# Gated scan and a sparse mixture of experts on one core: one chunk's statistics ahead of the others, two roots on GpSimd, and another weighting of the planned order

## The chip, the cores and the metric

The kernel runs on one core of a Trainium2 chip. The metric is the device time of one execution in microseconds (us). Before the change it is 376.28, the median of three runs that lie between 375.01 and 378.33. Besides these there is one execution under the hardware profiler; it took 377.76, and every duration of a single instruction below comes from it.

Engines go by these names: PE is TensorE's matmul pipeline and PEld its weight loads, DVE is VectorE, ACT is ScalarE, POOL is GpSimd, SP is SyncE, which here only issues transfers.

## The reference

The input `x` is 16 sequences of 256 tokens with 128 channels, 4096 rows of float32. Two sub-layers follow each other, both with a normalisation in front and one behind:

```
x = x + layernorm(scan(layernorm(x)))
x = x + layernorm(moe(layernorm(x)))

scan:  i = sigmoid(x Wi' + bi);  r = sigmoid(x Wr' + br)
       a = exp(-8 softplus(lambda) r);  g = sqrt(1 - a^2) (i x)
       h[t] = a[t] h[t-1] + g[t]          # along the 256 tokens

moe:   scores = sigmoid(x gate_w')         # 32 experts
       ids = top 4 of scores + e_bias;  w = scores[ids] / sum
       out = sum over e of combine[e] (silu(x w1[e]) * (x w3[e])) w2[e]   # 128 -> 96 -> 128
```

The four normalisations have no scale or offset. The reference computes all 32 experts for all tokens; only four of them have a weight that isn't zero.

## The kernel before

**Chunks.** The 4096 rows are eight chunks of 512, each four tiles of 128 rows. Every chunk goes through `mix` (from L578), which does the first sub-layer and the router: normalise (L589, on ScalarE or VectorE), transpose with TensorE (`swap`, L442), two gate matmuls (L600), tanh, exp, square, relu and square root on ScalarE (L607 to L625), products on VectorE (L621, L627), the scan along the tokens (L633, `hs`), transposes back (L641), the inner normalisation and the residual (L647), a second normalisation (`hn`), transposes again (`sw_c`), the router's logits (L675) and the top four.

**Statistics.** `norm` computes mean and variance for the first normalisation and is used twice: for chunk 0 alone, and for chunks 1 to 7 together. `rsqrt` (L385) computes 1/sqrt(var + eps) from them by nine small VectorE operations (L394 to L410), a shift of the bits and two Newton steps. A name in the list `POWS` would take another branch, which does it with an addition and a power on GpSimd (L391, L392); the list is empty. The roots are named by the normalisation and its chunk: `a0` and `a1` for the two of `norm`, `b` and a chunk for the one behind the scan, `c` and a chunk for the one ahead of the router, `d` for the last.

**Two ways through the experts.** Chunks 0, 2, 3 form group 0, chunks 4, 5, 6 group 1. Their rows are sorted by expert through DRAM: `send` (L499) has GpSimd scatter each tile of 128 rows four times by row numbers (L507, 16 indirect DMAs a chunk), SP loads the sorted blocks back (`loads`, L908), and `experts` (L912) works through 68 blocks per group in pieces of four: transposes (xT, L924), gate and up matmuls (gu, L938), silu on ScalarE (L944), product on VectorE (L946), transposes (aT, L954), down matmuls (y_ps, L964), a copy (yb, L973) and a store of 256 KB. Then `fetch` has GpSimd gather what belongs to each token (yk, L1044, 48 indirect DMAs a group) and `combine` adds it, normalises and stores (ff, L1080, L1082).

Chunks 1 and 7 aren't sorted. `dense` (L1089) computes all experts for them, in 24 tiles of 128 intermediate columns each: dg and du (gate and up) and dw (the combine weights spread over the columns) at L1111, silu on ScalarE (L1120), two products on VectorE (L1123, L1131), and the sum acc (L1135), whose matmuls all go into one bank. `finish` (L1142) transposes the sum back, normalises it, adds the residual (res) and stores it.

**The order of the work.** Each of these functions is a generator, and each `yield` announces one step: an engine, a planned duration in us, for ScalarE also the set of its function tables. `Order.run` (from L37) steps through all of them with a model of the engines' free times and writes the program's order from it: of the steps that can begin first (within `SOON` of each other on an engine) it takes the one with the smallest due time, where a ScalarE step that needs another table set counts `STAY` later. A step marked `EITHER` goes to ScalarE or VectorE, whichever the plan has finish it first; its two durations are given with it, and for the normalisations and the copies VectorE's are the constants `LND` and `CPD`. Due times come from the list `pieces` (L1180 on): `LEAD + STEP * c` for `mix` of chunk c, and from it those of `send`, `experts`, `find` and `fetch`; for the dense tiles `DUE`, `DDUE` and `DUE2`, and `KEEP` is how many dense tiles of the last chunk may be planned before the last expert piece of group 1 has begun (L1094). A step `UNTIL` waits in the plan for a time set by another step. What the generators call is issued in this order on PE, DVE, ACT and SP; each engine then runs its own list in order and waits for others by semaphores.

GpSimd's indirect DMAs have a pacing beside the data they need: `in_pace` (L489) makes each wait for the last matmul that the plan has `AHEAD` us or more earlier.

At the end, all engines load the flag `more` (L1233 on), which tells whether an expert has more rows than the planned blocks; a branch around the extra blocks follows.

Of the kernel before, what the change touches and what calls it, by code (L numbers as in the profile page):

```python
# [11 lines left out]
I32 = mybir.dt.int32  # L12
U32 = mybir.dt.uint32
AF = mybir.ActivationFunctionType
ALU = mybir.AluOpType
# [4 lines left out]
EPS = 1e-5  # L20
K = 4
GROUPS = ((0, 2, 3), (4, 5, 6))
DENSE = (1, 7)
# [5 lines left out]
PE, DVE, ACT, POOL, SP, TIME = "pe", "dve", "act", "pool", "sp", "time"  # L29
# [7 lines left out]
class Order:  # L37
# [37 lines left out]
    def due(self, rank, step):  # L75
        due, n = rank
        if isinstance(due, dict):
            due = due.get(step[0], due[None])
        return due + STAY * self.switches(step), n

    def run(self, pieces):
# [8 lines left out]
        while live:  # L90
# [14 lines left out]
            if kind in (PE, DVE, ACT, POOL, SP):  # L105
                soon = [r for r in ready if r[3][0] == kind and r[0] <= begin + SOON]
                begin, _, p, step = min(soon, key=lambda r: self.due(r[1], r[3]))
# [19 lines left out]
                live.remove(p)  # L127


POWS = ()  # L130
POOLW = 0.9
RATE = 1.29
AHEAD = 3.0
READ = 0.0
LAST = 2
TINY = 0.07
SOON = 0.1
STAY = 6.0
LEAD, STEP, PACE = 38.0, 13.0, 0.6
DUE = 70.0  # L140
DDUE = 1.0
DUE2 = 200.0
LND, CPD = 1.7, 0.9
FLY2 = 3
KEEP = 6
MORE = 20
REGS = 3
SBANKS = 6
# [2 lines left out]
SLOT, UNTIL = "slot", "until"  # L151
# [3 lines left out]
def tile_gated_scan_then_moe(  # L155
# [30 lines left out]
    nc = tc.nc  # L186
# [3 lines left out]
    N = B * T  # L190
    TPC = 4
    CH = TPC * P
# [6 lines left out]
    NW = [min(n, t * K // P + MORE) for n, t in zip(NB, TG)]  # L199
    QB = 4  # L200
# [178 lines left out]
    def rsqrt(rstd, var, pool, name):  # L379

        shape = [P, rstd.shape[1]]
        if name in POWS:  # L385
            v = pool.tile(shape, F32, tag="newt_v", name=f"nv_{name}")
            yield POOL, POOLW
            nc.gpsimd.tensor_scalar(v, var, EPS, None, ALU.add)
            nc.gpsimd.tensor_tensor(rstd, v, mhalf.to_broadcast(shape), ALU.pow)
            return  # L390
        v = pool.tile(shape, F32, tag="newt_v", name=f"nv_{name}")  # L391
        t = pool.tile(shape, F32, tag="newt_t", name=f"nt_{name}")  # L392
        yield DVE, TINY
        nc.vector.tensor_scalar(v, var, EPS, None, ALU.add)  # L394
        yield DVE, TINY
        nc.vector.tensor_scalar(
            t.bitcast(I32), v.bitcast(I32), 1, None, ALU.arith_shift_right
        )
        yield DVE, TINY
        nc.vector.tensor_scalar(  # L400
            rstd.bitcast(I32), t.bitcast(I32), -1.0, float(0x5F1FFFF9), ALU.mult, ALU.add
        )
        k = 0.703952253
        for square, plus in ((-1.0, 2.38924456), (-0.5 * k**3, 1.5 * k)):
            yield DVE, TINY
            nc.vector.scalar_tensor_tensor(t, rstd, square, rstd, ALU.mult, ALU.mult)
            yield DVE, TINY
            nc.vector.tensor_tensor(t, t, v, ALU.mult)
            yield DVE, TINY
            nc.vector.scalar_tensor_tensor(rstd, t, plus, rstd, ALU.add, ALU.mult)  # L410

    def moments(src, name, pool):

# [26 lines left out]
    times = {}  # L440
# [48 lines left out]
    def in_pace(ins):  # L489

        old = [b for at, b in beats if at <= order.now - AHEAD]
        if old:
# [6 lines left out]
    def send(g, cg):  # L499

        c = GROUPS[g][cg]
        yield UNTIL, lambda: times["rows", c][0] if ("rows", c) in times else None
        _, rows, hn = times["rows", c]
        for j in range(TPC):
            for k in range(K):
                yield POOL, RATE
                ins = nc.gpsimd.indirect_dma_start(  # L507
                    out=rows_in[g],
                    out_offset=bass.IndirectOffsetOnAxis(ap=rows[:, j, k : k + 1], axis=0),
                    in_=hn[:, j, :], in_offset=None,  # L510
                )
                apart(ins, f"in_{g}")
                in_pace(ins)
                sent[g].append(ins)
        times["sent", g] = order.now
        yield TIME, 2.5
        give("hn")
# [5 lines left out]

    def norm(chunks):

        for c in chunks:
            yield DVE, 1.1
            stats = small.tile([P, TPC, 6], F32, tag="stats_a", name=f"st_a{c}")
            for j in range(TPC):
                nc.vector.bn_stats(stats[:, j, :], x_all[:, c * TPC + j, :])  # L530
            for j in range(TPC):
                nc.vector.bn_aggr(mv_a[:, c * TPC + j, :], stats[:, j, :])
        span = slice(chunks[0] * TPC, (chunks[-1] + 1) * TPC)
        yield from rsqrt(rstd_a[:, span], mv_a[:, span, 1], const, f"a{chunks[0]}")
        yield DVE, TINY
        nc.vector.scalar_tensor_tensor(
            shift_a[:, span], mv_a[:, span, 0], -1.0, rstd_a[:, span], ALU.mult, ALU.mult
        )
        for c in chunks:
            times["normed", c] = order.now  # L540
# [337 lines left out]
    def loads(g, begin, end):  # L878

        yield UNTIL, lambda: (  # L880
            times["sent", g] if len(sent[g]) == len(GROUPS[g]) * TPC * K and g in tables else None
        )
        yield TIME, 2.5
        lists, _ = tables[g]
        for q in range(begin, end, QB):
            nb = min(QB, end - q)
            if (q - begin) % (QB * RB) == 0:
                n = min(QB * RB, end - q)
                yield SLOT, "regs"
                yield SP, 1.0  # L890
                _, rows = nc.values_load_multi_w_load_instructions(
                    lists[0:1, 0, q : q + n], engines={ET.SP}, min_val=0,
                    max_val=E * TG[g] - P,
                    skip_runtime_bounds_check_because="a block lies within its expert's rows",
                )
                yield PE, 0.6
                _, es = nc.values_load_multi_w_load_instructions(
                    lists[0:1, 1, q : q + n], engines={ET.PE}, min_val=0, max_val=E - 1,
                    skip_runtime_bounds_check_because="an expert's number",
                )  # L900
                for i in range(n):
# [187 lines left out]
    def dense(d, k):  # L1089
# [3 lines left out]
        _, hT = times["hT", c]  # L1093
        if d == len(DENSE) - 1 and k >= KEEP:  # L1094
            yield UNTIL, lambda: 0.0 if began[-1] * QB >= NW[-1] else None
# [75 lines left out]
    def spans(g, cg):  # L1171

        n = LAST if (g, cg) == (NG - 1, len(GROUPS[g]) - 1) else TPC
        return [(j, n) for j in range(0, TPC, n)]
# [2 lines left out]
    w1_f, w3_f = (w13[:, i].rearrange("h e i -> h (e i)") for i in range(2))  # L1177


    pieces = [(LEAD + STEP * c, mix(c)) for c in range(N // CH)]  # L1180
    pieces.append((0, norm(range(1))))
    pieces.append((-1, decays()))
    pieces.append((LEAD + STEP, norm(range(1, N // CH))))
    for g, chunks in enumerate(GROUPS):
        pieces += [(LEAD + STEP * c, send(g, cg)) for cg, c in enumerate(chunks)]
        full = LEAD + STEP * (chunks[-1] + 1)
        read = full + PACE * NW[g] + READ
        pieces.append((0, table(g)))
        pieces.append((0, loads(g, 0, NW[g])))
        pieces += [  # L1190
            (full + PACE * q, experts(g, q, NW[g])) for q in range(0, NW[g], QB)
        ]
        pieces += [
            (read + STEP * (cg + (j + n) / TPC), combine(g, cg, j, n))
            for cg in range(len(chunks)) for j, n in spans(g, cg)
        ]
        pieces += [(full + STEP * (cg + 1), find(g, cg)) for cg in range(len(chunks))]
        pieces += [
            (read + STEP * (cg + j / TPC), fetch(g, cg, j))
            for cg in range(len(chunks)) for j in range(TPC)  # L1200
        ]
    for d, c in enumerate(DENSE):
        pieces += [
            ({PE: 400 + d * UB + k, None: (DUE2 if d == len(DENSE) - 1 else DUE + DDUE * d * UB) + DDUE * k}, dense(d, k)) for k in range(UB)
        ]
# [13 lines left out]
    def step(piece, steps=None):  # L1219
# [60 lines left out]
```

## Time and profile before

| what | us |
|---|---|
| median of three runs | 376.28 |
| the profiled execution | 377.76 |
| its span, from the first to the last instruction | 376.1 |
| PE busy (1423 instructions) | 305.8, 81% |
| DVE busy (1252) | 290.7, 77% |
| ACT busy (376) | 201.6, 54% |
| POOL busy (220) | 195.4, 52% |
| mean granted clock of TensorE | 0.927 |

| where | us from the start |
|---|---|
| chunk 0's statistics end, its shift begins | 6.75, 17.31 |
| second chunk's first tanh | 32.72 |
| first dense tile (dg) | 56.34 |
| first send of rows | 66.30 |
| first expert transposes of group 0, its last down matmuls | 143.99, 223.92 |
| first gather of group 0, last | 229.82, 300.15 |
| last down matmuls of group 1 | 298.15 |
| first gather of group 1, last | 303.16, 363.09 |
| last matmul ends | 357.1 |
| last store issued, end of the span | 371.48, 376.1 |

The first table says that TensorE and VectorE are both busy for about four fifths of the span and that no engine is full all the time. The second table gives the stages, and a stage is what has to be read: which engine is full in it, and which wait ends last. Matmul records are pipelined, so that PE's busy time is not that of a TensorE at its peak. The granted clock is the share of full speed that the throttle allows TensorE; by slices it falls to 0.5 between 36 and 60 us.

In a line of the timeline the columns are the start, the duration, the engine, the source line, the operation, the tile written and those read, the number of instructions, and in square brackets the idle time of the engine before it with what ended that. In a table by stretches each engine has its busy us, with the number of instructions in brackets, in the order PE, PEld, DVE, ACT, POOL, and behind them the granted clock, the DMA share and GB/s.

### The profile page before, as it was taken

Reading aid. Unit: us, or ns where it says so; the run is one execution under the profiler, and the core shown is the slowest. Engines: PE = TensorE matmul, PEld = TensorE weight load, DVE = VectorE, ACT = ScalarE, POOL = GpSimd, SP = SyncE. Lnnn points to the kernel's source line nnn. Section 1 sums busy time; section 2 is a strip of 40 time slices with the busy share of each in tenths; the row PEclk is TensorE's granted clock in tenths of the full one; section 3 lists DMA queues with packets and bytes.
Section 4 is the critical chain, followed back from the end, with each engine's and each line's share of the span. In section 5 each row is a group of like instructions: output and inputs, shape, how many; then the busy total and the mean of one; then the engine's idle time right before and its main releaser. Section 6 shows DMA issues by size and latency. Waiting matters only on the chain.

```text
span 376.1 us, 6098 instructions
## 1 busy us (share of the span) xinstructions
PE 305.8 (81%) x1423; PEld 199.2 (53%) x1423; DVE 290.7 (77%) x1252; ACT 201.6 (54%) x376; POOL 195.4 (52%) x220
## 2 busy tenths in 40 slices
PE   1095479799999998888889989877999999999900
PEld 0051254354543446777889956766999644444300
DVE  6955996989899998877874799637367488796993
ACT  2289897688677415457565546545466523141210
POOL 5000000772777727656737504776377767777750
PEclk9998657699999999899999999999699999999975
DMA  6906678362111124455545255667374522122231
GB/s 150 315 0 183 195 207 200 99 195 84 45 56 49 56 72 141 140 161 173 160 133 155 75 166 158 181 182 196 89 200 121 161 69 78 52 56 77 56 101 31
DMA packets 78856, 47.16 MB, mean 125 GB/s; under 512 B 15296, under 2 KB 75744, under 8 KB 78816
## 3 DMA queue, kind: packets, MB, share of 16 engines
q1 hardware_dynamic: 53808, 25.05, 24.3%
q0 software_dynamic: 6144, 12.60, 11.8%
q10 hardware_dynamic: 18864, 9.08, 8.2%
q8 instruction: 13, 0.21, 0.2%
q14 instruction: 27, 0.22, 0.2%
HBM read 23.76 MB, written 22.94 MB: 124 GB/s over the span
## 4 chain that ended last, share of the span: by engine, by line
PE 62%; DVE 12%; issue 5%; ACT 3%; POOL 2%; DMA 1%; DVEq 0%; POOLq 0%
PE gu L938 12%; PE acc L1135 10%; PE dg L1111 8%; PE y_ps L964 8%; PE du L1111 8%; PE aT_ps L954 4%; PE xT_ps L924 4%; PE dw L1111 2%; PE pl L675 2%; POOL yk L1044 2%; DMA yk<-rows_out,slots 1%; DVE a L1131 1%; DVE a L1123 1%; PE pr L600 1%; PE sw_c L448 1%
## 5 line engine op out<-in xcount | busy, mean ns | idle before, releaser
L507 POOL DMA_INDIRECT rows_in<-hn,rows x96 | 94.9, 988 | 113.2 <-DVE tot L481 60.8
L1044 POOL DMA_INDIRECT yk<-rows_out,slots x96 | 95.7, 996 | 54.8 <-issue 17.4
L938 PE MATMUL gu<-w,xT 128*128 x272 | 53.8, 336 | 7.9 <-issue 6.4
L1120 ACT ACTIVATE a<-dg 128x512 f32<-128x512 f32 x48 | 28.4, 596 | 49.7 <-PE dg L1111 49.2
L1135 PE MATMUL acc<-a,w_all 128*128 128x512 f32 x96 | 50.5, 617 | 3.3 <-DVE a L1131 1.4
L938 PEld LDWEIGHTS gu<-w,xT 128*128 128x128 f32 x272 | 44.6, 194 | 12.4 <-issue 7.7
L1111 PE MATMUL dg<-hT,w 128*128 128x512 f32 x96 | 50.7, 614 | 0.0
L1111 PE MATMUL du<-hT,w 128*128 128x512 f32 x96 | 50.0, 606 | 0.0
L946 DVE TENSOR_TENSOR act<-act,gu 128x192 f32<-128x192 f32 x68 | 23.0, 349 | 23.0 <-ACT act L944 22.5
L964 PE MATMUL y_ps<-w_sb,aT 96*128 x272 | 36.2, 280 | 5.3 <-issue 3.2
L1131 DVE TENSOR_TENSOR a<-a,dw 128x512 f32<-128x512 f32 x48 | 32.5, 681 | 9.1 <-PE dw L1111 8.6
L964 PEld LDWEIGHTS y_ps<-w_sb,aT 96*128 96x128 f32 x272 | 34.5, 196 | 8.5 <-issue 7.5
L1123 DVE TENSOR_TENSOR a<-a,du 128x512 f32<-128x512 f32 x48 | 32.4, 678 | 4.9 <-ACT a L1120 3.3
L944 ACT ACTIVATE act<-gu 128x192 f32<-128x192 f32 x68 | 22.0, 330 | 25.8 <-PE gu L938 21.6
L973 ACT COPY yb<-y_ps 128x512 f32<-128x512 f32 x34 | 19.9, 586 | 23.3 <-PE y_ps L964 22.3
L1135 PEld LDWEIGHTS acc<-a,w_all 128*128 128x128 f32 x96 | 17.1, 195 | 23.9 <-DVE a L1131 9.2
L1111 PEld LDWEIGHTS dg<-hT,w 128*128 128x128 f32 x96 | 18.3, 196 | 19.0 <-issue 17.3
L1111 PEld LDWEIGHTS du<-hT,w 128*128 128x128 f32 x96 | 17.7, 195 | 15.5 <-issue 14.0
L954 PE MATMUL aT_ps<-ident,act 128*96 128x128 f32 x136 | 20.4, 279 | 2.3 <-issue 1.6
L370 ACT COPY aT<-aT_ps 96x512 f32<-96x512 f32 x29 | 16.6, 583 | 9.4 <-PE aT_ps L954 8.1
L1054 DVE TENSOR_TENSOR yk<-yk,wk 128x512 f32<-128x512 f32 x24 | 16.5, 688 | 6.2 <-DMA yk<-rows_out,slots 6.0
L370 ACT COPY xT<-xT_ps 128x512 f32<-128x512 f32 x29 | 16.7, 588 | 7.0 <-PE xT_ps L924 6.1
(215 smaller groups left out, 520.9 us busy)
## 6 DMA issues: line engine op xcount, KB each, us to landing
xb<-rows_in SPq DMA_DIRECT2D x136, 64.0 KB
rows_out<-yb ACTq DMA_DIRECT2D x34, 256.0 KB
rows_in<-zeros SPq DMA_DIRECT2D x8, 512.0 KB
w<-in_L_ffn_w_dram SPq DMA_DIRECT2D x8, 384.0 KB
x_all<-in_L_attn_x_dram SPq DMA_DIRECT2D x8, 256.0 KB
w_all<-in_L_ffn_w_dram SPq DMA_DIRECT2D x4, 384.0 KB
w_sb<-in_L_ffn_w_dram SPq DMA_DIRECT2D x4, 384.0 KB
rows_in<-hn,rows POOLq DMA_INDIRECT x96
```

The lines of the kernel that those rows point to most:

```text
L370: (nc.vector.tensor_copy if kind == DVE else nc.scalar.copy)(dst, src)
L507: ins = nc.gpsimd.indirect_dma_start(out=rows_in[g], out_offset=bass.IndirectOffsetOnAxis(ap=rows[:, j, k : k + 1], axis=0), in_=hn[:, j, ...
L938: nc.tensor.matmul(pg[:, b, :], lhsT=xT[:, (h + b) * P : (h + b + 1) * P], rhs=w13[:, :, bass.ds(e, 1), :].rearrange("h s o i -> h s (o i) ...
L946: nc.vector.tensor_tensor(act[:, h : h + m, :], act[:, h : h + m, :], pg[:, :m, I : 2 * I], ALU.mult)
L954: nc.tensor.transpose(pa[:I, b * P : (b + 1) * P], act[:, b, :], ident)
L964: ins = nc.tensor.matmul(py[:, b, :], lhsT=aT[:, b * P : (b + 1) * P], rhs=w2_sb[:, bass.ds(e, 1), :].rearrange("i o h -> i (o h)"), start ...
L1044: ins = nc.gpsimd.indirect_dma_start(out=yk[:, k, :], out_offset=None, in_=rows_out[g], in_offset=bass.IndirectOffsetOnAxis(ap=rows[:, j, ...
L1111: ins = nc.tensor.matmul(ps, lhsT=lhsT, rhs=rhs, start=True, stop=True)
L1120: nc.scalar.activation(a, pg, AF.Silu)
L1123: nc.vector.tensor_tensor(a, a, pu, ALU.mult)
L1131: nc.vector.tensor_tensor(a, a, pw, ALU.mult)
L1135: nc.tensor.matmul(accs[d], lhsT=w2_all[:, k, :], rhs=a, start=(k == 0), stop=(k == UB - 1))
```

## The change

Eleven constants of the plan and three pieces of code differ.

- `rsqrt`: the roots of `b1` and `c1`, chunk 1's two inner normalisations, go to GpSimd (`POWS`), with a planned 1.4 instead of 0.9. A name in the new list `ATONCE` (`a0`, chunk 0's root) has its nine operations issued in one step of 1.7, where each was a step before, between which the plan could put others.
- `norm` of chunks 1 to 7 waits in the plan until chunk 0's shift is written.
- Chunk 7's `mix` is due at 200 (`MIXD`) instead of 38 + 13 x 7 = 129.
- `AHEAD` is 5 instead of 3.
- `STEP` 11 instead of 13, `DUE` 62 instead of 70, `DDUE` 2 instead of 1, `SOON` .12 instead of .1, `STAY` 8 instead of 6.
- `LND` 1.1 instead of 1.7, `CPD` .7 instead of .9: VectorE is planned to be quicker at normalisations and copies.
- `KEEP` 0 instead of 6.
- `LATER` is 0 and adds nothing.

```diff
-POWS = ()
-POOLW = 0.9
+POWS = ("b1","c1")
+ATONCE = ("a0",)
+POOLW = 1.4
 RATE = 1.29
-AHEAD = 3.0
+AHEAD = 5.0
+MIXD = 200.0
+LATER = 0.0
...
-SOON = 0.1
-STAY = 6.0
-LEAD, STEP, PACE = 38.0, 13.0, 0.6
-DUE = 70.0
-DDUE = 1.0
+SOON = 0.12
+STAY = 8.0
+LEAD, STEP, PACE = 38.0, 11.0, 0.6
+DUE = 62.0
+DDUE = 2.0
...
-LND, CPD = 1.7, 0.9
+LND, CPD = 1.1, 0.7
...
-KEEP = 6
+KEEP = 0
...
     def rsqrt(rstd, var, pool, name):
...
-        yield DVE, TINY
-        nc.vector.tensor_scalar(v, var, EPS, None, ALU.add)
-        yield DVE, TINY
...
+        def steps():
+            nc.vector.tensor_scalar(v, var, EPS, None, ALU.add)
+            yield
...
+        if name in ATONCE:
+            yield DVE, 1.7
+            for _ in steps():
+                pass
+            return
         yield DVE, TINY
+        for _ in steps():
             yield DVE, TINY
...
     def norm(chunks):
 
+        if chunks[0]:
+            yield UNTIL, lambda: times.get(("normed", 0))
...
-    pieces = [(LEAD + STEP * c, mix(c)) for c in range(N // CH)]
+    pieces = [
+        (MIXD if c == DENSE[-1] else LEAD + STEP * c, mix(c)) for c in range(N // CH)
+    ]
```

In the program that the planner writes with these, 30 normalisations of 128x128 and 14 copies of 128x512 have moved from ScalarE to VectorE, ScalarE has 24 loads of function tables instead of 27, and all 24 dense tiles of chunk 7 stand behind the experts of group 1 on TensorE, where before the sums of three stood ahead of the last of them. Of chunk 7's `mix`, the transposes and the logits stand later among the experts. Chunk 7's last addition (res) and its store stand behind the load of `more` and a branch; before, they stood ahead of it.

More of the change, by code (lines that the diff above doesn't have):

```diff
@@ L392, in rsqrt @@
         t = pool.tile(shape, F32, tag="newt_t", name=f"nt_{name}")
-        yield DVE, TINY
-        nc.vector.tensor_scalar(v, var, EPS, None, ALU.add)
-        yield DVE, TINY
-        nc.vector.tensor_scalar(
-            t.bitcast(I32), v.bitcast(I32), 1, None, ALU.arith_shift_right
-        )
-        yield DVE, TINY
[L400 to L404, printed above, removed]
-            yield DVE, TINY
[L406 to L410, printed above, removed]
+        def steps():
+            nc.vector.tensor_scalar(v, var, EPS, None, ALU.add)
+            yield
+            nc.vector.tensor_scalar(
+                t.bitcast(I32), v.bitcast(I32), 1, None, ALU.arith_shift_right
+            )
+            yield
+            nc.vector.tensor_scalar(
+                rstd.bitcast(I32), t.bitcast(I32), -1.0, float(0x5F1FFFF9), ALU.mult, ALU.add
+            )
+            k = 0.703952253
+            for square, plus in ((-1.0, 2.38924456), (-0.5 * k**3, 1.5 * k)):
+                yield
+                nc.vector.scalar_tensor_tensor(t, rstd, square, rstd, ALU.mult, ALU.mult)
+                yield
+                nc.vector.tensor_tensor(t, t, v, ALU.mult)
+                yield
+                nc.vector.scalar_tensor_tensor(rstd, t, plus, rstd, ALU.add, ALU.mult)
+        if name in ATONCE:
[3 more added lines that the diff above has]
+            return
+        yield DVE, TINY
+        for _ in steps():
+            yield DVE, TINY
     def moments(src, name, pool):
@@ L1190, in tile_gated_scan_then_moe @@
         pieces += [
-            (full + PACE * q, experts(g, q, NW[g])) for q in range(0, NW[g], QB)
+            (full + PACE * q + LATER * g, experts(g, q, NW[g])) for q in range(0, NW[g], QB)
         ]
```

## The prediction

> **What bounds the kernel now.** First the end, in the chain of waits followed back and the timeline, since a time is decided there; then the busy time by stretches, to see which engine carries each stage.
>
> ```profile
> 229.82 0.98 POOL L1044 DMA_INDIRECT yk<-rows_out,slots  x1 [16.29 <-DMA xb<-rows_in]
> ...
> 266.82 0.95 POOL L1044 DMA_INDIRECT yk<-rows_out,slots  x1 [3.21 <-PE y_ps L964]
> ...
> 303.16 0.94 POOL L1044 DMA_INDIRECT yk<-rows_out,slots  x1 [2.06 <-PE dw L1111]
> ...
> 363.09 0.95 POOL L1044 DMA_INDIRECT yk<-rows_out,slots  x1 [0.30 <-issue]
> ...
> 371.03 0.42 DVE L1080 TENSOR_TENSOR ff<-ff,x_all 128x256 f32<-128x256 f32 x1 [0.94 <-ACT ff L377]
> 371.48 0.37 SPq L1082 DMA_DIRECT2D out_dram<-ff  x1
> ```
>
> These are the first gather of group 0, one that was held, the first and the last of group 1, and the end. The last expert block's y_ps of group 1 begins at 298.15; its result has to be copied, stored and landed, and 5.0 us later the first of 48 gathers goes. The 48 take 59.9 (1.25 each), the last sums and norm 8.4, and the span ends 4.6 after the last store, when it has landed. TensorE runs beside this: from 298.15 it has 56.25 us of dense tiles of chunk 7 at full clock and ends them at 357.1, 58.95 for 56.25. It is the second, nearly as late, way to the end: chunk 7's normalisation ends at 364.3, 7.2 after its last matmul.
>
> ```profile
> 20.00:40.00 20.00, 12.78 (x36) 5.81 (x36) 11.25 (x41) 19.33 (x31) 0.00 (x0) 0.86 0.37 99
> 60.00:80.00 20.00, 17.25 (x55) 7.92 (x54) 16.47 (x91) 12.57 (x25) 10.65 (x11) 0.79 0.46 134
> 100.00:120.00 20.00, 19.62 (x61) 8.33 (x60) 19.18 (x91) 16.51 (x21) 15.12 (x17) 1.00 0.16 52
> 300.00:320.00 20.00, 20.00 (x52) 8.88 (x51) 16.68 (x46) 6.31 (x12) 13.89 (x14) 1.00 0.28 73
> 360.00:376.00 16.00, 0.00 (x0) 0.00 (x0) 9.82 (x49) 1.75 (x4) 3.12 (x4) 0.56 0.21 58
> ```
>
> Columns: busy PE, PEld, DVE, ACT, POOL, then granted clock. ScalarE is full at 20 to 40, TensorE from 80 to 140 and again from 300, with VectorE 0.8 us from full at 100 to 120; after 360 TensorE is idle. So the end is y_64 of group 1 (298.15) plus the longer of two tails.
>
> **The change, part by part.** *Start of chunk 0.*
>
> ```profile
> 17.31 0.16 DVE L536 SCALAR_TENSOR_TENSOR shift_a<-mv_a,rstd_a 128x4 f32<-128x4 f32 x1
> 17.51 1.65 ACT L377 ACTIVATE xn<-x_all,shift_a,rstd_a 128x128 f32<-128x128 f32 x4 [6.77 <-DVE shift_a L536]
> 20.76 3.19 ACT L377 ACTIVATE xn<-x_all,shift_a,rstd_a 128x128 f32<-128x128 f32 x8 [0.45 <-DVE shift_a L536]
> ```
>
> Chunk 0's statistics are ready at 6.75, yet its shift comes at 17.31, since its root's nine small operations are mixed among the other chunks' statistics. In one piece, behind the decay operations: shift near 9.8, 7.5 earlier. The others' statistics wait for it and their shift moves from 20.54 to about 24.2. ScalarE fills its 6.8 idle with chunk 0's gates, but the second chunk needs the others' shift: its first tanh, at 32.72, I place at 30.8, a gain of **2**. Bounds: 3.7 lost (all later chunks follow the late shift) to 7.5 gained (all follow chunk 0). The mixing steps also release 22 weight loads and zero fills on SP, five per chunk (L621 to L650), so these come as much earlier; chunk 7 has none left to move.
>
> *Roots of chunk 1 on GpSimd.* Two pairs of operations replace 18 on VectorE, 1.76 per root at the 0.2 us steps in which such chains run. No row shows a power; GpSimd's nearest are a memset at .10, a 128x32 copy at .92, and an indirect DMA at 1.71. A pair costs .2 to 3.4: 1.6 gained to 1.7 lost per root, on the latency of a dense chunk whose tiles are not due yet. I take 0, the copy's row (2 x .92) being equal to what goes. GpSimd is idle for 60.8 before its first send (66.30), so that hides them; behind them stand the sends, late if a root waits beyond that point.
>
> [...]
>
> *ScalarE to VectorE.* The planned prices move 30 normalisations (128x128: .48 each on ScalarE; on VectorE 16 of hn are busy 4.4, .27 each) and 14 copies (.59 against .69): VectorE gets 30 x .27 + 14 x .69 - 18 x .2 = +14, of which 5.6 stand ahead of the first gated product L946 of group 0 and about 7 ahead of group 1's end. ScalarE loses three table loads of 1.283 (27 to 24), but between the second chunk's first tanh and the first dense silu it has seven in both. The cover is VectorE's idle time: it is busy 75.66 of the 84 us from 60 to 144, so 8.3 are free for 5.6. At nothing then; without the cover, 5.6.
>
> *TensorE's order.* This is the main term. Nothing is removed; pieces move behind the experts. At full clock (dense gate, up and down tiles .86 each, the small dw .22, transposes .435 per four, logits .83) the work ahead of group 0's first expert transposes falls by 2.15, ahead of group 0's last y_ps by 6.4, and ahead of group 1's last y_ps by **8.4** (215.7 to 207.3): chunk 7's transposes and logits go later, all its 24 dense tiles too, where now three have their sums in before group 1 ends. TensorE is the busy engine there, so y_64 goes from 298.15 - 8.4 - 2 = 287.75. What left comes behind it: 56.25 + 8.4 = 64.65.
>
> *More slack for indirect DMAs.* Group 0's 48 gathers take 73.3 against 59.9 for group 1's, and 9.6 of that are waits for a PE instruction planned too close, the held row above among them. With 5 instead of 3 us between, they shrink; but group 0's gathers gain slack here, not the end: the first of group 1 is already bound by 298.15 + 5.0. At nothing; if the last gather of group 0 stays where it is (300.15), the first of group 1 goes at 294.8 at the earliest instead of 292.75, 2.0 lost. Of group 1's own gathers all but 1.8 and .9 of the waits are the .3 of an issue.
>
> *Program end.* In the changed order chunk 7's last addition and store stand behind the load of the flag `more` and a branch; now ff's last store is the last before it. No row has a branch. The store costs from .37 (one issue) to 4.62 (SP first waits until ff's store has landed, as the end of the span does). I take **2.5**, midway, since nothing nearer shows.
>
> *Sum.* GpSimd's way: first gather 287.75 + 5.0 = 292.75, last 352.7, last store 361.1, with two additions of chunk 7 mixed in (.35 each) 361.8. TensorE's way: 64.65 x 58.95/56.25 = 67.75, ending at 355.5; normalised 7.2 later, 362.7, added (.7) 363.4. The later one, plus 2.5, plus 4.62: a span of 370.5. The profiled execution took 377.76 for a span of 376.1, 1.66 around it: 372.2. It lies .4% above the median of the runs (376.28), so **370.7** for a median.
>
> **The rivals.** (a) *Chunk 0's lead carries through*: the tiles follow chunk 0 by 7.5 instead of 2. For it: ScalarE's 6.77 idle. Against: the others' shift later, and the granted clock near .5 at 36 to 60. Both ways to the end move 5.5: 365.2.
>
> (b) *Holes instead of a shorter stage*: the dense tiles that leave the expert stage filled gaps in it (TensorE is 17.4 to 17.8 of 20 at 160 to 200), and half of the 8.4 is not got. y_64 at 291.95; TensorE's way then decides: 291.95 + 67.75 + 7.2 + .7 + 2.5 + 4.62 = 374.7, a median of 374.9. What left must still be done later, which takes the gain back.
>
> (c) *VectorE becomes the bound, slower than before*: at 100 to 140 it has .8 to 1.0 idle in 20, and the 5.6 that are put ahead of the first gated product delay every expert block; the tiles that left then make holes only. It decides as soon as more than 5.6 of the 8.3 idle cannot be used, that is when fewer than 5.6 fall between the added operations. y_64 at 298.15 - 2 + 5.6 = 301.75; 67.75 + 7.2 + .7 + 2.5 + 4.62 behind it: 384.5, a median of 384.7.
>
> (d) *The slack does not do what it says*: 119 gathers and sends wait for TensorE now, 117 in the changed order, so they can be held as before. It costs the 2.0 above on GpSimd's way, .4 on the sum, and lies within the forecast.
>
> **How the numbers follow.** Forecast .47 (367 to 373.5 by the ends of the program-end term, 2.1 either side, and rival d), (a) .12, (b) .22, (c) .19. The range takes in (a) and (b) and reaches to (c): 361 to 384; outside remain some .12 above and .04 below. A measurement of this kernel tells about 1% from no change, 372.5 to 380.0: faster .42 + .12 + .03 = .57, same .05 + .17 = .22, slower .02 + .19 = .21.
>
> **What would show it.** Right: chunk 0's shift near 9.8 and the second chunk's first tanh near 31; y_64 of group 1 near 288; the last gather near 353; last matmul near 355; a store behind the branch 2 to 3 us after ff's. The groups must show waits of a gather for y_ps or dw below the 9.6 of group 0. Wrong: idle TensorE between pieces at 140 to 280 with y_64 above 292 is (b); VectorE at 20 of 20 from 60 to 140 with the first expert transposes later than 143.99 is (c); a GpSimd power of over 3 us, or sends later than 66.30, overturns the second part; a TensorE clock below 1.00 at 300 to 355 stretches the longer tail.

## The result and the profile after

The changed kernel takes 378.24 us, the median of 14 runs (376.83 to 380.01); the kernel before takes 376.27 in the runs beside it. The ratio is 1.006, with a 95% interval of 1.0035 to 1.0084: not faster, and by that interval about half a per cent slower, where 370.7 was predicted. Its profiled execution took 379.9 for a span of 378.0.

The timeline of the changed kernel, at the places that were shown of the kernel before:

```profile
9.73 0.15 DVE L551 SCALAR_TENSOR_TENSOR shift_a<-mv_a,rstd_a 128x4 f32<-128x4 f32 x1
22.26 1.65 ACT L380 ACTIVATE xn<-x_all,shift_a,rstd_a 128x128 f32<-128x128 f32 x4 [2.21 <-DVE shift_a L551]
...
299.19 0.94 POOL L1059 DMA_INDIRECT yk<-rows_out,slots  x1 [4.42 <-DMA rows_out<-yb]
...
359.04 1.05 POOL L1059 DMA_INDIRECT yk<-rows_out,slots  x1 [0.30 <-issue]
...
363.70 1.12 PE L1150 MATMUL acc<-a,w_all 128*128 128x512 f32 x2 [1.25 <-DVE a L1146]
...
373.87 0.69 DVE L1180 TENSOR_TENSOR res<-res,x_all 128x512 f32<-128x512 f32 x1 [2.25 <-DVEq L1255]
374.59 0.37 SPq L1182 DMA_DIRECT2D out_dram<-res  x1
```

Chunk 0's shift comes at 9.73, as reckoned, and the last gather 4.05 earlier than before. But the last of chunk 7's sums on TensorE ends at 364.8 instead of 357.1 (called the last matmul's end here, as ahead of the prediction). TensorE's way to the end, which was the shorter one before, is now the longer: chunk 7's normalisation, addition and store follow it to 378.0.

The busy times of the two stages behind the first expert transposes, from there to group 1's last y_ps (y_64 in what follows) and from there to the last matmul's end (columns as before: PE, PEld, DVE, ACT, POOL, granted clock, DMA share, GB/s); first of the kernel before:

```profile
143.99:298.15 154.16, 137.62 (x930) 121.36 (x928) 106.95 (x453) 86.11 (x188) 91.52 (x92) 0.97 0.55 155
298.15:357.12 58.97, 57.96 (x150) 25.17 (x148) 48.56 (x137) 16.86 (x33) 43.37 (x45) 1.00 0.25 65
```

and of the changed kernel:

```profile
140.17:294.25 154.08, 133.33 (x909) 120.50 (x908) 110.89 (x450) 77.45 (x167) 84.11 (x87) 0.96 0.53 149
294.25:364.85 70.60, 67.26 (x171) 28.45 (x169) 59.03 (x178) 16.73 (x30) 47.10 (x49) 1.00 0.25 66
```

The expert stage is as long as it was, though TensorE has less to do in it. It sits idle for 154.08 - 133.33 = 20.75 instead of 16.54. What left the stage came back behind it, 9.3 us of busy time, with 3.3 of idle in the place of 1.0.

Beside three of the experiments the changed kernel took 378.76 (ratio 1.013, 1.003 to 1.022). In its profile there (span 375.4) the stage is 152.16 long, with 20.98 idle. So two profiles of one kernel differ by 2 to 3 us in y_64 and in the span, and the idle time is what they share.

```profile
139.56:291.72 152.16, 131.18 (x907) 118.77 (x908) 110.44 (x444) 76.95 (x167) 84.01 (x87) 0.97 0.53 150
```

Three of the runs below leave TensorE's order in this stage as it is (`AHEAD` back, and two at the program's end). Over all five profiles the idle time of the stage is 20.7 to 21.2, while y_64 lies between 291.2 and 294.7. What differs is the granted clock: the stage is 151.0 long with two stretches of 3.4 us at half clock in it, 152.2 and 152.5 with three, 153.8 and 154.1 with four. The kernel before has three in its profile.

### The profile page after: what moved, and what is told of

Its sections match the earlier page's. It is cut to its first block, busy times and chain, and to the rows that moved or that the text cites. A ratio compares the mean times of both kernels' runs of the same rounds, so it can differ in the third digit from the quotient of the medians.

```text
span 378.0 us, 6109 instructions
## 1 busy us (share of the span) xinstructions
PE 308.0 (81%) x1423; PEld 202.5 (54%) x1423; DVE 303.7 (80%) x1278; ACT 180.1 (48%) x329; POOL 196.3 (52%) x224
## 5 line engine op out<-in xcount | busy, mean ns | idle before, releaser
L1059 POOL DMA_INDIRECT yk<-rows_out,slots x96 | 93.1, 970 | 57.0 <-issue 17.1
L953 PE MATMUL gu<-w,xT 128*128 x272 | 56.6, 349 | 11.3 <-issue 11.2
L953 PEld LDWEIGHTS gu<-w,xT 128*128 128x128 f32 x272 | 47.2, 204 | 14.0 <-issue 13.0
L961 DVE TENSOR_TENSOR act<-act,gu 128x192 f32<-128x192 f32 x68 | 23.2, 347 | 24.4 <-ACT act L959 24.2
L1126 PEld LDWEIGHTS dg<-hT,w 128*128 128x128 f32 x96 | 18.6, 197 | 21.2 <-issue 18.5
L1126 PEld LDWEIGHTS du<-hT,w 128*128 128x128 f32 x96 | 17.6, 193 | 16.6 <-issue 14.8
L969 PE MATMUL aT_ps<-ident,act 128*96 128x128 f32 x136 | 19.6, 273 | 5.1 <-issue 2.9
L939 PE MATMUL xT_ps<-ident,xb 128*128 128x128 f32 x136 | 20.8, 284 | 0.0
L373 ACT COPY aT<-aT_ps 96x512 f32<-96x512 f32 x24 | 13.6, 584 | 13.4 <-PE aT_ps L969 13.1
```

The costliest lines, as they stand in the source:

```text
L939: nc.tensor.transpose(pt[:, b * P : (b + 1) * P], xb[:, b, :], ident)
L953: nc.tensor.matmul(pg[:, b, :], lhsT=xT[:, (h + b) * P : (h + b + 1) * P], rhs=w13[:, :, bass.ds(e, 1), :].rearrange("h s o i -> h s (o i) ...
L961: nc.vector.tensor_tensor(act[:, h : h + m, :], act[:, h : h + m, :], pg[:, :m, I : 2 * I], ALU.mult)
L1059: ins = nc.gpsimd.indirect_dma_start(out=yk[:, k, :], out_offset=None, in_=rows_out[g], in_offset=bass.IndirectOffsetOnAxis(ap=rows[:, j, ...
L1126: ins = nc.tensor.matmul(ps, lhsT=lhsT, rhs=rhs, start=True, stop=True)
```

## The experiments

**What are the idle stretches?** The list of waits of TensorE in the expert stage, in the kernel before and then in the changed one:

```profile
PE gu L938 <- issue: 6.4, 3, 2.7
PE y_ps L964 <- issue: 3.2, 2, 1.7
```

```profile
PE gu L953 <- issue: 11.2, 4, 3.9
PE aT_ps L969 <- issue: 2.9, 2, 2.1
```

"issue" is a wait for nothing that the profile shows. The view of the tile `lists`, which holds the sorted blocks' row and expert numbers, shows what TensorE's sequencer (PEldq in its lines) does meanwhile, here in the changed kernel, with minimum, median and maximum in ns:

```profile
L906 SPq TENSOR_LOAD <-lists x12: 522/756/1056, 116.6 to 269.0; - x12
L912 PEldq TENSOR_LOAD <-lists x12: 2267/3228/5568, 122.8 to 273.4; - x12
```

Each of 12 loads brings 12 expert numbers into registers (the last of each group 8) and takes 2.27 to 5.57 us. The longest one and the matmul behind it:

```profile
L912 PEldq TENSOR_LOAD <-lists x1: 5568/5568/5568, 164.0 to 164.0; - x1
169.75 0.42 PE L953 MATMUL gu<-w,xT 128*128 x1 [3.92 <-issue]
```

The load runs from 164.0 to 169.6, and TensorE's next matmul begins at 169.75; matmuls already issued cover the first 1.8 us, and 3.92 stay idle. Laid over TensorE's gaps, nearly all idle time of the stage stands beside these loads, 19.2 us in the changed kernel and 16.9 in the one before (counted from the first load on, which lies ahead of the first expert transposes). The theory from here on is "holes": the loads stop TensorE, and the tiles that the change moved away stood where they covered some of that. It was tried from several sides.

**Short loads in the changed kernel** (and, as the second run, in the kernel before):

```diff
-    RB = 3
+    RB = 1
-REGS = 3
+REGS = 6
```

> The changed kernel with TensorE's and SyncE's expert numbers loaded for each piece (4 values a load, 34 loads, six sets of registers) instead of three pieces at once (12 values, 12 loads of 2.27 to 5.57 us). The planner reorders other work with it. Theory 'holes': a load's time goes by its values, a third each, some 1.1 us, which the matmuls already issued hide; the holes of 2 to 4 us go and with them the half-clock stretches behind them; idle time of TensorE from the first expert transposes to y_64 of group 1 falls from 20.8 to below 12, y_64 of group 1 comes 4 to 8 earlier and the time falls by 2 to 6. Rival 'fixed price': each load takes some 3 us whatever its length; 34 of them stop TensorE for 100 us in all, idle time grows above 30 and the time by 10 or more.

Measured: 372.12, ratio .988 (.982 to .994). The view of `lists` and TensorE's waits in the stage:

```profile
L912 PEldq TENSOR_LOAD <-lists x34: 995/1018/1602, 123.2 to 268.1; - x34
```

```profile
PE aT_ps L969 <- DVE act L961: 1.9, 3, 0.7
PE y_ps L979 <- ACT aT L373: 1.9, 3, 1.4
```

A load of four values takes 1.02, a third of 3.1 to 3.2: .25 a value, and no fixed price to speak of. The sum of all loads hardly changes (40.8 with long ones, 37.9 with short ones), yet the idle time falls from 20.75 to 10.06: of the 40.8 us TensorE sat idle in 17.6, of the 37.9 in 4.9, and the rest lay behind matmuls already issued. The stage takes 145.51, y_64 comes at 286.08, 8.2 earlier. The largest waits left are of one expert step for another. The theory holds, and the rival with a fixed price falls. The stage with short loads:

```profile
140.57:286.08 145.51, 135.45 (x916) 116.38 (x915) 106.11 (x441) 81.95 (x177) 80.34 (x82) 0.99 0.55 156
```

> The kernel before with expert numbers loaded for each piece (4 values, 34 loads) as in the run on the changed kernel, nothing else. Theory 'holes': in the kernel before 16.9 of the 16.5 us that TensorE idles in the expert stage stand beside register loads, against 19.2 in the changed kernel; with short loads both lose most of it, y_64 of group 1 comes 4 earlier than 298.15 although 3.9 us of dense tiles more stand ahead of it, and the time is 370 to 372, within 1 of the changed kernel with short loads (372.1): then the change is worth nothing without the long loads and its loss comes from how the loads fall. Rival 'the change is worse for another reason' (the tail behind the experts): this one is 3 or more faster than the changed kernel with short loads, 369 or less. Rival 'the change gains and the holes hid it': this one stays at 374 or more.

Measured: 371.50, ratio .990 (.984 to .995); y_64 at 290.43, the stage 147.33 with 7.07 idle:

```profile
143.10:290.43 147.33, 140.26 (x941) 118.80 (x940) 108.34 (x449) 92.09 (x202) 92.93 (x94) 1.00 0.57 164
```

Without the long loads the change is worth nothing measurable: .990 against .988, each beside the kernel before; with four runs each, the intervals of ±.006 can't tell more. The short loads don't take away all that the change adds: it has 4.2 us more idle time in the stage than the kernel before with long loads, and still 3.0 more with short ones (10.06 against 7.07). There y_64 is 4.35 earlier with the change, and the last matmul's end 10.7 later (355.98 against 345.30).

**Back to KEEP = 6 in the changed kernel.**

```diff
-KEEP = 0
+KEEP = 6
```

> The changed kernel with KEEP = 6 again, nothing else. On TensorE 4.9 us of dense tiles of chunk 7 (two dg, two du, three dw, one sum) go back ahead of group 1's last y_ps. Theory 'holes': in the expert stage TensorE idles 20.8 us, mostly behind its register loads (12 of 2.3 to 5.6 us), and the tiles fill such holes. Then y_64 of group 1 comes at most 1.5 later than 294.25, the last matmul about 4 to 5 earlier than 363.7 (near 359), and the time falls by 3 to 4, to 374 or 375, where GpSimd's way (span 374.0 by the changed kernel's last gather) takes over. Rival 'full array': every us of tiles put back delays the experts by the same; y_64 near 299, the last matmul where it is, first gather of group 1 near 304, and the time 378 to 380.

Measured: 379.39, ratio 1.007 (1.003 to 1.011). y_64 came at 298.06, 3.8 later, and the last matmul's end at 360.55, 4.3 earlier; GpSimd's last gather went from 359.04 to 363.18. So 4.9 us put back cost 3.8 where they went and saved 4.3 where they came from; the holes swallowed 1.1. (Both profiles have four stretches at half clock in the stage, and 298.06 lies outside the 291.2 to 294.7 of the unedited order.) The rival "full array" is the nearer one: two ways to the end exchange their places and the time stays.

**The same step the other way, with short loads**, in the kernel before:

```diff
-    RB = 3
+    RB = 1
-REGS = 3
+REGS = 6
-KEEP = 6
+KEEP = 0
```

> The kernel before with expert numbers loaded for each piece and KEEP = 0, on the same chip. Theory: with short loads TensorE's work moves one for one, y_64 of group 1 some 5 to 7 earlier than with short loads alone (290.43), and GpSimd's way with it, TensorE's having 10 to spare: .970 to .982 of the kernel before, faster than both and than short loads alone (.990). Rival: the first gather of group 1 is held by the last of group 0, or the tiles filled the rest of the holes: .985 or more.

Measured: 368.63, ratio .982 (.974 to .990); its figure on another chip is told below. y_64 came at 287.11 against 290.43, 3.3 earlier for 7.1 us moved and not the 5 to 7 of the theory, the last gather 3.7 earlier and the last matmul's end 4.1 later. The stage's idle time rose from 7.07 to 10.87; no stretch at half clock falls into the stage in either profile.

```profile
143.09:287.11 144.02, 133.15 (x921) 115.01 (x920) 106.34 (x446) 89.28 (x196) 92.79 (x94) 1.00 0.59 168
```

So even with short loads the tiles had covered holes, and more than half of what leaves the stage, 3.8 of 7.1, stays behind in it as idle time. TensorE's longest waits there:

```profile
PE aT_ps L954 <- DVE act L946: 3.4, 5, 1.3
PE gu L938 <- ACT act L944: 1.2, 1, 1.2
```

These are waits of one expert step for the next, which the dense tiles had filled. The step pays here all the same, since TensorE's way had 10 us to spare and GpSimd's way bound the time.

**The other parts, each undone in the changed kernel.** The due time of chunk 7's mixing steps (`MIXD` gone, so 115):

```diff
-        (MIXD if c == DENSE[-1] else LEAD + STEP * c, mix(c)) for c in range(N // CH)
+        (LEAD + STEP * c, mix(c)) for c in range(N // CH)
```

> The changed kernel with chunk 7's mixing steps due at LEAD + 7 * STEP = 115 instead of 200, nothing else. Chunk 7's transposes and logits go back ahead of most of group 0's experts: TensorE's work ahead of group 0's last y_ps grows by 2.3, ahead of group 1's by 1.1. Theory 'holes': it fills holes only, y_64 of group 1 within 1 of 294.25 and the time within 1 of the changed kernel's 378. Rival 'MIXD made the loss' (chunk 7's latency inside the expert stage holds TensorE): the time falls by 2 or more.

Measured: 383.25, ratio 1.021 (1.014 to 1.028). Neither: it is slower. y_64 came at 292.33, within what profiles of the unedited order show, but behind it TensorE waited for the product on VectorE:

```profile
PE acc L1150 <- DVE a L1146: 5.5, 5, 1.7
```

5.5 instead of 3.3. The profiled execution, at 380.55, is the fastest of its four runs and doesn't show the rest.

The slack:

```diff
-AHEAD = 5.0
+AHEAD = 3.0
```

> The changed kernel with AHEAD = 3 again: the order on TensorE, VectorE and ScalarE is the same, only the matmuls that indirect DMAs wait for are later ones. Theory: the slack acts on sends and on group 0's gathers, which are not what the end waits for: y_64 of group 1 within 1 of 294.25, the first gather of group 1 within 1 of 299.19, the time within 1 of the changed kernel's 378.2. Rival 'the slack gains': the sends of chunks 2 and 3 (first at 82.1 and 107.5, with waits of 10.2 and 5.2 for TensorE) come 2 later or more, with them the first expert transposes (140.17), and the time rises by 2. Rival 'the slack loses' (transfers run into TensorE's work): the time falls by 1 or more.

Measured: 377.95, ratio 1.007 (1.004 to 1.011), nothing that can be told from the changed kernel. The sends of chunks 2 and 3 began at 81.8 and 107.2 against 82.1 and 107.5. y_64 came 3.1 earlier than in the changed kernel's first profile, but .6 from its second (291.72): the spread of profiles of one order.

The planned prices on VectorE:

```diff
-LND, CPD = 1.1, 0.7
+LND, CPD = 1.7, 0.9
```

> The changed kernel with the planned prices of normalisations and copies on VectorE as before (LND 1.7, CPD .9), so that the planner gives ScalarE its share back. The planner then also begins the experts of group 0 with 17 us less TensorE work ahead of them (dense tiles of chunk 1 go behind). Theory 'holes and a conserved sum': the tiles moved back come between the experts or behind them; the last matmul stays within 3 of 363.7 and the time within 3 of 378. Rival 'VectorE was the loss': TensorE's waits for the product a (L1146) in the tail go, 3.3 in the changed kernel, and the time falls by 3 or more.

Measured: 394.61, ratio 1.050 (1.043 to 1.057). Both expectations miss. The first expert transposes came at 137.41, only 2.8 earlier for 17 us less ahead of them: TensorE sat idle for 40.3 from its first matmul to there, against 27.6. y_64 came at 294.82, no earlier than in the changed kernel, and the last matmul's end at 379.6, 14.8 later. Tiles moved out of a stage became idle time in it and work behind it, once more and at a larger size. Giving ScalarE its share back doesn't win the loss back; with the other new constants the cheap prices are worth 16 us. What VectorE's added work costs by itself can't be read from this run, since the planner's whole order moved with the prices.

**The start alone**, in the kernel before: chunk 0's root in one step and the other chunks' statistics behind it, as in the change.

> The kernel before with one part of the change alone: chunk 0's root in one step, and the other chunks' statistics behind it. Theory: chunk 0's shift near 9.8, the others' near 22, the first expert transposes of group 0 some 3 to 4 us earlier than 143.99 (in the changed kernel 3.8), and all of it kept to the end, since both ways to the end begin behind the experts: time 373 to 374. Rival 'lost in the expert stage': group 1's y_64 within 1 of 298.15 and the time 376 to 378.

Measured: 378.65, ratio 1.009 (1.005 to 1.012), slightly slower. In the profile the first transposes came at 141.86, 2.1 earlier, y_64 1.6 earlier (with two stretches at half clock in the stage instead of three), the last gather 2.1 earlier; yet the end came at 376.6 against 376.1, since behind the last gather VectorE now had chunk 7's normalisation in the middle of the last sums (15.6 from the last gather to the end, 13.0 before). With short loads:

> The kernel before with short loads (one piece each) and the start of the change alone (chunk 0's root in one step, the other chunks' statistics behind it). With long loads the start alone gained 1.6 at y_64 of group 1 and nothing at the end. Theory 'the holes ate the lead': with short loads the 4.6 us of TensorE's work that go from ahead of the first expert transposes to behind them don't make holes, the lead of 2 to 4 reaches the end, .975 to .985 of the kernel before against .990 for short loads alone. Rival 'the lead is lost at the end or never there' (the other chunks' shift comes later, 22 to 24 against 20.5): .988 to 1.00.

Measured: 373.47, ratio .994 (.989 to .998), by its bounds the lead is lost. Its profile shows where: the first transposes come at 138.44, 4.7 earlier than with short loads alone, but y_64 at 291.56, 1.1 later. Holes don't explain that (idle time 5.9 against 7.07). TensorE is busy for 147.24 us in the stage instead of 140.26: work that had stood ahead of the first transposes stands behind them.

> The same with KEEP = 0 as well (short loads, the change's start, no dense tile of chunk 7 before the last expert piece). Short loads with KEEP = 0 alone gave .982. If the lead reaches the end, .970 to .978, the fastest of all; if it is lost, .980 to .990.

Measured: 367.39, ratio .978 (.974 to .982), the fastest of all kernels here, 8.4 below the kernel before beside it; against the same without the start (.982) the intervals overlap, though in the profiles y_64 comes 4.8 earlier (282.28 against 287.11).

**The program's end.** The flag was made to wait for chunk 7's addition:

```diff
-        nc.vector.tensor_tensor(res, res, x_all[:, c * TPC : (c + 1) * TPC, :], ALU.add)
+        ends.append(nc.vector.tensor_tensor(res, res, x_all[:, c * TPC : (c + 1) * TPC, :], ALU.add))
...
-    nc.vector.tensor_tensor(more, behind[0], behind[1], ALU.max)
+    after(nc.vector.tensor_tensor(more, behind[0], behind[1], ALU.max), ends[-1:])
```

> The changed kernel, in which the flag for the extra blocks is computed behind chunk 7's last addition, so that this addition and its store come ahead of the flag's load and the branch again; the order is otherwise the same. In the changed kernel the addition waits 2.25 for the load on VectorE and the store goes at 374.59. Theory: the store goes at 372.4, the loads and the branch follow while it lands, the time falls by 1 to 2. Rival: the loads and the branch then follow the store and cost the same behind it; time within .5 of the changed kernel.

Measured: 385.02, ratio 1.024 (1.019 to 1.029), 7 slower than the changed kernel. Both expectations fall. The last store went at 374.28, and the span ended at 385.7. The view of the branch's line there:

```profile
L1256 PEldq COMPARE_BRANCH  x1: 3807/3807/3807, 374.9 to 374.9; - x1
L1256 DVEq COMPARE_BRANCH  x1: 72/72/72, 375.1 to 375.1; - x1
```

TensorE's branch takes 3.8 and the end comes 7 after it. In the kernel before and the changed one TensorE loads the flag at 358.0 and 365.5, and the jump lies beside the normalisations. The branch takes 3.79 in the changed kernel, but not always: in the kernel before it is

```profile
L1238 PEldq COMPARE_BRANCH  x1: 368/368/368, 358.4 to 358.4; - x1
```

What fills those 7, and why the same branch takes .37 in four of the profiles here and 3.3 to 3.8 in the others, was not settled.

Then the flag, its loads, the branch and the extra blocks were left out, in the changed kernel and in the one before. On one chip the kernel before takes 442.36 instead of 376, so that what was measured there stands only against each other:

> The changed kernel without its last part: no flag, no loads of it, no branch and no extra blocks behind it (the work for an expert with more rows than the planned blocks is left out; these inputs don't need it). All else is the same order. In the changed kernel VectorE's normalisation of chunk 7 ends at 371.62, the addition comes at 373.87 behind VectorE's jump, its store at 374.59, the end at 378.0. Theory 'program end': the addition follows at once, the store near 372.4, the span ends near 375.5; time 2 to 3 less than 378.2. Rival: the end waits for something else (the last landings, TensorE's jump), time within 1.

> The kernel before without the same part. Its last store goes at 371.48 and the span ends 4.62 later. Theory 'program end is what the change added': here the jump lies beside the store's landing, the time falls by less than 1.5, to 374.5 or more; then without the branch the changed kernel and the one before are equal within 1. Rival 'both pay the same': it falls by 2 to 3 as the changed kernel does, and the .6% between them stays, to be looked for ahead of the end.

> The kernel before with expert numbers loaded for each piece (371.5) and KEEP = 0 as well: 7.1 us of TensorE's work (dense tiles of chunk 7) go from ahead of group 1's last y_ps (290.43) to behind the experts. With the holes gone, TensorE's work should move one for one. Theory: y_64 of group 1 near 283.5 to 285, the last gather near 350, the last matmul at 345 to 347; GpSimd's way, which bounds that kernel (last gather 356.48, end 369.3), comes 5 to 6 earlier, TensorE's way has 10 to spare: time 365 to 367, faster than both kernels and than both with short loads. Rival: the first gather of group 1 is held by the last of group 0 (286.10 there) or the tiles filled the rest of the holes: time 370 or more.

Measured there: 1.029 (1.022 to 1.035), 1.001 (.995 to 1.007) and .983 (.976 to .989) of the kernel before. On another, where the kernel before takes 376.05, with the changed kernel beside them:

> The changed kernel itself, unedited, so that the three runs beside it can be held against it on the same chip. Expected .6% above the kernel before, as at first, if the program runs on a chip where that takes 376; on the chip where it took 442 no figure for it exists, and the change without the branch was 2.9% above the kernel before: there I expect 2 to 4% above.

> The changed kernel without the flag, its loads, the branch and the extra blocks (left out: the work for experts with more rows than the planned blocks), beside the changed kernel on one chip. Theory 'program end': 2 to 3 us faster than the changed kernel, its store at once behind the addition. Rival 'the end waits for something else': within 1.

> The kernel before without the same part, on the same chip. Theory 'the jump lies beside the landing there': within 1.5 of the kernel before (1.0008 of it on the slower chip). Rival 'both pay': 2 to 3 less.

Measured: 378.76 for the changed kernel, 378.64 without the branch (ratio 1.012, 1.003 to 1.020) and 374.25 for the kernel before without it (.997, .993 to 1.001). By the medians, taking the jump out gains nothing in the changed kernel and at most .7% in the one before. In the profile the addition then follows its normalisation at once, but the last matmul ended 3 later than in the profile beside it (365.2 against 362.2), so that the theory's 2 to 3 us are not to be seen in the time; from the last matmul's end to the end of the span it is 11.4 against 13.2. By the medians the loss isn't made by the jump.

## Why the prediction was wrong

**The step that failed is TensorE's order: "y_64 goes from 298.15 - 8.4 - 2 = 287.75".** It came at 294.25, in the second profile at 291.72. Against the forecast span of 370.5 the profiled 378.0 is 7.5 late, and that is 6.5 at y_64, 2.85 in the tail up to the last matmul (70.60 against 67.75), and 1.9 the other way behind it (13.1 against 15.0). In the second profile it is 4.9 late: 4.0, 2.7 and 1.8 the other way.

- **The 6.5.** The first transposes were near the mark (140.17 against 143.99 - 2.15 - 2 = 139.84). From there the stage was to shrink by 8.4 - 2.15 = 6.25 and didn't. 4.2 of that is added idle time, which every profile of this order has. The other 2 are mostly busy time at half clock: the second profile, with one such stretch less, has 2 us less of busy time. The table by stretches shows how a hole was paid twice around the longest load of the changed kernel:

```profile
166.00:170.00 4.00, 0.25 (x1) 0.26 (x2) 1.00 (x3) 0.14 (x1) 3.08 (x4) 1.00 0.90 266
170.00:173.40 3.40, 3.40 (x12) 3.40 (x12) 0.91 (x3) 1.27 (x3) 2.49 (x4) 0.51 0.37 116
```

  TensorE is idle for 3.9, and for the next 3.4 it is full at half the clock. A hole of 2.6 (180.4 to 183.0) was followed by such a stretch too, from 183.7 to 187.1 at .50; one of 2.1 that ended at 263.4 wasn't (1.00 from there to 266.8). What ties the clock to the hole was not shown.

- **What I read wrongly in the profile.** TensorE's order was costed by taking its work out at full clock, because TensorE "is the busy engine there". It is busy for 137.62 of 154.16; the rest are gaps that stay when work goes. The runs put a number on it: 4.9 us back in cost 3.8, 7.1 out (with short loads) gained 3.3, 6.25 out in the change itself shortened the stage by .1 to 2. Rival (b), "holes instead of a shorter stage", had the mechanism with half of 8.4 kept, 374.9, and it had .22 where the forecast had .47. Its y_64, 291.95, lies within the 291.2 to 294.7 of the five profiles; it missed the longer tail, and the slower clock of some executions. Most of the idle time that was there before the change, the register loads, stood in the profile of before as "issue" and was not looked into: with short loads both kernels are 4 to 6 faster. But of the 4.2 that the change adds, 3.0 stay with short loads. By the waits listed there that part is of one expert step for another, and the run with short loads and `KEEP` at 0 shows the same for the dense tiles alone.

- **The tail.** Of 2.85, 2.3 are TensorE waiting for VectorE's product (3.3 against 1.0). Why the product comes later is not shown: VectorE is busy for 59.03 of 70.60, hardly a larger share than before (48.56 of 58.97). Not all of chunk 7's dense tiles stand behind the experts, as was written ahead of the result: the gate matmuls of two (dg) and the up matmuls of one (du) ran ahead of y_64.

- **The early start**: shift at 9.73 as predicted, the second chunk's first tanh at 29.25 instead of 30.8. The step was right in its place and worth nothing at the end by itself, as the run with the start alone shows. The others' shift came at 22.04 instead of about 24.2.

- **The roots on GpSimd** took .24 + 1.05 and .23 + 1.47, from the first operation's start to the second's end 1.37 and 1.79, against an estimated 1.76 on VectorE: nothing, as taken. The power itself costs 1.05 and 1.47, so that the price taken for a pair from the row of a copy (2 x .92) was near.

- **VectorE's 14 us** cost nothing that could be found ahead of the tail, and rival (c) with the experts starting later didn't occur (140.17 is earlier). **The slack** costs nothing and gains nothing, as forecast (group 0's gathers take 70.3 from first to last, not 73.3; that reached to group 1's first). **The program's end** was sized at 2.5 + .7 and took 2.97 from normalisation to store. That is luck: 2.5 was the middle between two bounds, and "No row has a branch" is wrong, since the trace of before has one on each engine. Without the branch the time stays.

What stays open is why one load took 5.57 and another 4.12 instead of the median's 3.2. It isn't chance: in the second profile the same two took 5.59 and 4.35. The longest of the twelve had the busiest DMA engines beside it (share .94 from 164.0 to 169.6), but the next one had .59, and no run tested it. Open is also which of the planner's new constants puts the loads where less covers them: neither `KEEP` nor `MIXD` alone brings the old idle time of 16.5 back (19.4 and 20.6).

## What to carry to other kernels

Before work is moved out of a "full" stage, subtract its busy time from its length and find what the idle part is; if it stays when the work goes, the move only lengthens what comes after. A wait that a profile puts down to "issue" can have its cause in the sequencer, as here (the seven of the changed kernel's expert stage, 15.5 us, each ended with a register load): look for such loads on that queue, and make a long one into short ones that already issued work covers (here the idle time fell from 20.75 to 10.06). With two ways to the end that lie within a few us, a shift of work from one to the other gains at most the difference.

## What the hardware showed

- TensorE's register loads of `lists` took .25 us a value (by their medians, 12 values 3.1 to 3.2, 4 values 1.02) and SyncE's .06 to .08 (.75 and .30).
- The jump over the block of extra experts took TensorE's sequencer 3.3 to 3.8 us for the branch alone in eleven profiles and .37 in four. In the run with the flag behind chunk 7's addition the program's end came 10.8 after the branch was begun (374.9 to 385.7). VectorE's first instruction behind its branch came 3.0 after it in the changed kernel (370.89 to 373.87).
- One chip ran the kernel before in 442 instead of 376 us.
